# An MLP over q and the routing of a mixture of experts: fixed instruction orders, a halved last group, and a first load in two parts

## The chip, the cores and the metric

The kernel runs on one core of one Trainium2 chip. A core has a matrix engine (TensorE, PE in the profile), a vector engine (VectorE, DVE), an engine for activation functions (ScalarE, ACT), a general engine (GpSimd, POOL) that here mostly issues indirect transfers, and a sync engine (SyncE, SP) that issues plain transfers. Each engine runs its own list of instructions in order, and the engines wait for one another by semaphores. The metric is the device time in microseconds (us), from launch to end, and less is better. All data are float32.

## The reference

The reference is two layers of a network on x of 8 x 512 tokens of 128 values, thus 4096 tokens: a convolution stage, a feed-forward stage with quantized values, a stage that trains a small MLP on the keys and applies it to the queries, and a mixture of experts. The change touches the end of the third stage and the beginning of the fourth:

```
h_q = swish(q @ gate) * (q @ val)              # hidden size 512
x = x + h_q @ proj @ proj_w + proj_b
xt = layernorm(x).reshape(T, 128)
logits = xt @ Wg + bg                          # 8 experts
gate_vals, exp_idx = top_k(softmax(logits), 2)
gate_vals = gate_vals / sum(gate_vals)
eidx = exp_idx.T.reshape(-1)
oh = one_hot(eidx, 8)
pos = sum((cumsum(oh, axis=0) - oh) * oh, axis=-1)
keep = pos < 1229                              # the capacity of one expert
buf[eidx, pos] += where(keep, xt, 0)           # rows of the first choices of all tokens come first
h = gelu(einsum("ecd,edf->ecf", buf, W1) + b1)
ye = einsum("ecf,efd->ecd", h, W2) + b2
x = x + sum over the two choices of ye[eidx, pos] * gate_vals * keep
```

A row's place in its expert's buffer depends on how many earlier tokens chose that expert; rows of second choices are placed from the other end, so that one count per expert is enough.

## The kernel before

The kernel runs `sequence_conv`, `fp4_ffn`, `ttt` and `moe` one after the other. Tokens lie in tiles of P = 128; G = 4 tiles are a group of W = 512 columns, and there are NG = 8 groups. The last part of `ttt` (L853 to L877), "the MLP on q", loops over the groups. For each of NF = 4 chunks of the hidden size it has two matmuls into PSUM buffers of 512 columns, `pa` (L857) and `pb` (L861), of which there are four; ScalarE makes silu of `pa` into `sw` (L865, two buffers) and VectorE the product into `ht` (L866). These are called chunk 0 to chunk 3 here. Then sixteen matmuls of 128 columns, four chunks into each of the group's four tiles, make the output `o` (L872), and VectorE adds it to x (L876, "the x add").

Between the products and the output of group g stands `moe.route(g - 1)` (L1198 to L1288), the routing of the group before; the last group's routing follows the loop (L877). A route has these parts:

- turn: four transposes of x (L1212), copied to `xt` by ScalarE (L1214)
- statistics: `bn_stats` and `bn_aggr` by tile (L1217, L1218), then `rsqrt` by a bit trick and three Newton steps (13 small VectorE operations, L85 to L93)
- logits: four matmuls of 8 columns (L1224), made into `lg` on VectorE (L1226, L1227)
- rows: the normalized tokens into `xr` (ScalarE, L1231), with a copy for the second choice (VectorE, L1252)
- choices: for each of the two, five operations that find the best expert and its one-hot `hot` (L1237 to L1241); the tanh of the difference gives both weights (L1247 to L1250)
- counts: `hot` is counted up over the group's tiles into `cum`, starting from `seen`, the count of all earlier groups (L1254 to L1260); this is what ties each route to the one before it
- sums: two matmuls over the partitions (L1261, L1262) into `pos`, which shares a PSUM tile named `both` with the logits
- places: seven operations that turn the sums into row numbers `slot` (L1263 to L1273)
- scatters: eight indirect transfers on POOL (L1278), one for each tile and choice, second choices (k = 1) before first ones (k = 0). Each k = 0 scatter waits until the k = 1 scatters of the route before have landed (`self.after`, L1286).

The eight scatters of one route are called a train here. `Moe.experts` (L1297) then goes over the E = 8 experts: SP loads an expert's nine full row tiles in one transfer and its last, ragged tile in another (L1333, L1337), both after all scatters; then transposes (L1356), a copy (L1358), first matmuls `ph` (L1362), Gelu (L1365), second matmuls `po` (L1371), the results (L1380, L1384) and the scatter of results (L1386).

In which order an engine runs its instructions is not written out in this part: the compiling framework places every instruction on its engine by its own plan, so that parts of a route stand between the products and outputs of the loop. A class `Line` is there already (it keeps the instructions handed to it in the order of the calls, without a semaphore), and other stages use it; this part does not.

Of the kernel before, what the change touches and what calls it, by code (L numbers as in the profile page):

```python
# [1 line left out]

# [14 lines left out]
P = 128  # L17
# [706 lines left out]
def ttt(cx):  # L724
# [10 lines left out]
    with ExitStack() as st:  # L735
# [106 lines left out]
        with ExitStack() as s4:  # L842
# [10 lines left out]
            for g in range(NG):  # L853
                ht = p2.tile([P, NF, W], F32, tag="ht", name="ht")
                for c in range(NF):
                    pa = ps_h.tile([P, W], F32, tag="h", name="pa")
                    nc.tensor.matmul(  # L857
                        pa, gate[:, c * P : (c + 1) * P], qt[:, g * W : (g + 1) * W], start=True, stop=True
                    )
                    pb = ps_h.tile([P, W], F32, tag="h", name="pb")  # L860
                    nc.tensor.matmul(  # L861
                        pb, val[:, c * P : (c + 1) * P], qt[:, g * W : (g + 1) * W], start=True, stop=True
                    )
                    sw = p2.tile([P, W], F32, tag="sw", name="sw")
                    nc.scalar.activation(sw, pa, AF.Silu)  # L865
                    nc.vector.tensor_tensor(ht[:, c, :], pb, sw, ALU.mult)  # L866
                if g:
                    moe.route(g - 1)
                o = ps_o.tile([P, G, D], F32, tag="o", name="o")
                for j in range(G):  # L870
                    for c in range(NF):
                        nc.tensor.matmul(  # L872
                            o[:, j, :], ht[:, c, j * P : (j + 1) * P], w2[:, c, :],
                            start=(c == 0), stop=(c == NF - 1),
                        )
                nc.vector.tensor_tensor(grp(cx.x, g), o, grp(cx.x, g), ALU.add)  # L876
            moe.route(NG - 1)  # L877
# [251 lines left out]

class Moe:  # L1130
# [67 lines left out]
    def route(self, g):  # L1198
        cx = self.cx
        nc, tc, p2 = cx.nc, cx.tc, self.p2  # L1200
        vec = nc.vector

        def small(tag, *shape, dt=F32):
            return p2.tile([P, *shape], dt, tag=tag, name=tag)

        def over_e(t):
            return t.unsqueeze(2).to_broadcast([P, G, E])

        x, at = grp(cx.x, g), slice(g * G, (g + 1) * G)
        tp = self.ps_t.tile([P, G, P], F32, tag="t", name="tp")  # L1210
        for j in range(G):
# [234 lines left out]
```

## Time and profile before

| | us |
|---|---|
| median of three runs (lowest, highest) | 1364.11 (1363.63, 1365.26) |
| the profiled execution | 1367.42 |
| its span, first to last instruction | 1365.7 |
| TensorE, VectorE, ScalarE, POOL busy in the whole span | 1122.8, 776.2, 493.7, 761.5 |
| mean granted TensorE clock of the span | 0.927 |

One row of the page's list of the costliest groups bears on the part in question, and so does its line of the granted clock:

```profile
PEclk9888899976999999999999999999999886899996
...
L1278 POOL DMA_INDIRECT rows<-xr,slot x64 | 62.4, 976 | 104.9 <-DVE rs L93 55.6
```

A row reads: line, engine, operation, output and inputs by the program's names, count; then busy time in all and mean ns of one; then the idle time just ahead of the group on its engine and what ended most of it. The clock line has 40 slices of 34 us; a digit is the clock that TensorE was granted, in tenths of full speed. The slices of the part that the change touches read 9, 8, 8, 6, 8, between two rows of nines near the right end: in the trace it runs from 1004 us, when the loop over the groups begins, to 1167 us, when the first expert's rows have landed.

A row of the timeline gives start and duration in us, engine, line, operation and shapes, with count, and in brackets the idle time ahead of it and what ended it.

### The profile page before, as it was taken

To read this page: it belongs to the slowest core of one execution; us is meant where nothing else is said; L and a number is where in the kernel's file an instruction comes from. 1 tells how busy PE (TensorE), PEld (TensorE's weight loads), DVE (VectorE), ACT (ScalarE), POOL (GpSimd) and SP (SyncE) were. 2 spreads that over 40 slices of the span, in tenths; PEclk is the share of its full clock that TensorE was granted. 3 is DMA by queue.
4 is the path that set the end of the run, shared out by engine and by line. 5 is a ranking of instruction groups with operands and counts; after the bars stand their busy time and mean duration, and the time that the engine had idled before them with its cause. 6 is when DMAs were issued, how large, how long until landed. Compare 5 with 4: busy or idle time off the path is not lost.

```text
span 1365.7 us, 15325 instructions
## 1 busy us (share of the span) xinstructions
PE 1122.8 (82%) x5211; PEld 661.2 (48%) x5211; DVE 776.2 (57%) x1754; ACT 493.7 (36%) x1002; POOL 761.5 (56%) x724
## 2 busy tenths in 40 slices
PE   4688888726878689999998999999898873799981
PEld 1233333314656445555556455555665442576761
DVE  8689899978796544444445444444556564122233
ACT  4534455325555632222234222222442221333320
POOL 4336566644554588888841888888104336244533
PEclk9888899976999999999999999999999886899996
DMA  4322223924000000000000000000000001222146
GB/s 133 90 73 73 73 73 95 348 82 143 1 0 1 0 0 1 0 0 1 1 1 1 1 0 1 0 1 1 0 1 30 24 28 43 57 60 63 48 114 182
DMA packets 61614, 63.07 MB, mean 46 GB/s; under 512 B 6767, under 2 KB 44478, under 8 KB 61536
## 3 DMA queue, kind: packets, MB, share of 16 engines
q1 hardware_dynamic: 54016, 52.37, 13.1%
q0 software_dynamic: 4608, 8.43, 2.0%
q10 hardware_dynamic: 2912, 1.29, 0.4%
q8 instruction: 41, 0.67, 0.2%
q14 instruction: 37, 0.30, 0.1%
HBM read 37.90 MB, written 25.04 MB: 46 GB/s over the span
## 4 chain that ended last, share of the span: by engine, by line
issue 62%; PE 10%; DMA 2%; DVE 1%; SPq 1%; POOL 1%; POOLq 0%; ACT 0%; another core or an unknown queue 0%; DVEq 0%
PE po L1371 5%; PE ph L1362 5%; DMA w<-in_L_ffn_W 1%; POOL last L1386 1%; DMA y<-last 1%; PE tp L1356 0%; POOLq L1442 0%; DVE ye L1380 0%; DVE xt L1358 0%; DMA xe<-rows 0%; DMA L_ffn_bg<-in_L_ffn_bg 0%; SPq L604 0%; SPq L710 0%; DMA last<-ye,tok 0%; SPq L59 0%
## 5 line engine op out<-in xcount | busy, mean ns | idle before, releaser
L1051 POOL TENSOR_TENSOR ds<-sw,s 128x512 f32<-128x512 f32 x64 | 81.4, 1272 | 86.7 <-DVE sw L1046 86.7
L1278 POOL DMA_INDIRECT rows<-xr,slot x64 | 62.4, 976 | 104.9 <-DVE rs L93 55.6
L1386 POOL DMA_INDIRECT res<-ye,xe x70 | 68.2, 974 | 89.6 <-DVE ye L1384 36.3
L1053 POOL TENSOR_TENSOR ds<-ds,s 128x512 f32<-128x512 f32 x64 | 112.1, 1751 | 5.0
L391 PE MATMUL cv<-pr,sel 128*32 128x512 f32 x512 | 78.4, 691 | 22.5 <-DVE pr L381 22.4
L1044 ACT COPY b<-pb 128x512 f32<-128x512 f32 x64 | 37.4, 585 | 162.1 <-PE pb L1040 161.6
L1365 ACT ACTIVATE ht<-ph,b 128x512 f32<-128x512 f32 (+1 forms) x96 | 55.5, 602 | 107.9 <-PE ph L1362 96.5
L1048 DVE TENSOR_TENSOR h<-sw,b 128x512 f32<-128x512 f32 x64 | 50.2, 784 | 70.6 <-ACT b L1044 70.1
L1371 PEld LDWEIGHTS po<-w,ht 128*128 128x128 f32 (+1 forms) x640 | 79.5, 193 | 15.3 <-issue 9.5
L1052 POOL TENSOR_TENSOR ds<-sw,ds 128x512 f32<-128x512 f32 x64 | 82.5, 1289 | 5.0
L1371 PE MATMUL po<-w,ht 128*128 128x128 f32 (+1 forms) x640 | 83.0, 284 | 2.7 <-ACT ht L1365 2.6
L1054 POOL TENSOR_TENSOR ds<-ds,b 128x512 f32<-128x512 f32 x64 | 81.4, 1271 | 5.0
L1076 PEld LDWEIGHTS pp<-proj,ht 128*128 128x128 f32 x512 | 67.1, 191 | 30.7 <-issue 29.8
L1362 PE MATMUL ph<-xt,w 128*128 128x512 f32 (+1 forms) x192 | 73.9, 522 | 9.6 <-DVE xt L1358 7.6
L383 POOL TENSOR_TENSOR pr<-base,en 128x512 f32<-128x512 f32 x48 | 69.6, 1479 | 21.7 <-ACT en L345 21.7
L381 DVE TENSOR_TENSOR pr<-base,w 128x3072 f32<-128x3072 f32 x24 | 79.6, 3318 | 2.5 <-ACT w L343 2.5
L1380 DVE TENSOR_TENSOR ye<-po,b 128x512 f32<-128x512 f32 (+2 forms) x32 | 14.9, 488 | 112.7 <-PE po L1371 87.1
L1046 DVE TENSOR_TENSOR sw<-pa,s 128x512 f32<-128x512 f32 x64 | 44.2, 691 | 53.6 <-ACT s L1042 53.6
L1071 ACT COPY ht<-pt 128x512 f32<-128x512 f32 x64 | 37.4, 585 | 101.6 <-PE pt L1069 101.6
L1086 PE MATMUL ph<-proj_t,dpt 128*128 128x512 f32 x128 | 71.6, 641 | 0.0
L1088 DVE TENSOR_TENSOR db<-ph,sw 128x512 f32<-128x512 f32 x64 | 44.2, 691 | 47.4 <-PE ph L1086 47.4
L1038 PE MATMUL pa<-gate,kt 128*128 128x512 f32 x128 | 66.8, 604 | 2.5 <-ACT b L1044 2.4
(320 smaller groups left out, 2665.0 us busy)
## 6 DMA issues: line engine op xcount, KB each, us to landing
base<-far SPq DMA_DIRECT2D x64, 268.0 KB
rows<-empty SPq DMA_DIRECT2D x1, 5005.0 KB
xe<-rows SPq DMA_DIRECT2D x8, 585.0 KB
res<-zero SPq DMA_DIRECT2D x1, 4096.0 KB
w<-in_L_ffn_W SPq DMA_DIRECT2D x16, 256.0 KB
y<-res SPq DMA_DIRECT2D x16, 256.0 KB
far<-avg SPq DMA_DIRECT2D x8, 272.0 KB
x<-in_L_attn_x SPq DMA_DIRECT2D x8, 256.0 KB
```

Of the source, the lines that this page charges most:

```text
L381: vec(nc.vector.tensor_tensor(pr[:, :nv, :], s["base"][:, :nv, at], w.to_broadcast([P, nv, L]), ALU.mult))
L383: nc.gpsimd.tensor_tensor(pr[:, d, :], s["base"][:, d, at], s["en"][:, g, :], ALU.mult)
L391: ten(nc.tensor.matmul(s["cv"][32 * j : 32 * (j + 1), :], sel[:, i].rearrange("p a h -> p (a h)"), s["pr"][g][:, i * NJ + j, :], start=(g ...
L1051: nc.gpsimd.tensor_tensor(ds, sw, s, ALU.mult)
L1052: nc.gpsimd.tensor_tensor(ds, sw, ds, ALU.subtract)
L1053: nc.gpsimd.tensor_tensor(ds, ds, s, ALU.add)
L1054: nc.gpsimd.tensor_tensor(ds, ds, b, ALU.mult)
L1076: nc.tensor.matmul(pp, ht[:, c * P : (c + 1) * P], proj[:, c, :], start=(c == 0), stop=(c == NF - 1))
L1086: nc.tensor.matmul(ph, dpt, proj_t, start=True, stop=True)
L1362: nc.tensor.matmul(ph[:, :n], self.w1[:, e, c * P : (c + 1) * P], xt[:, :n], start=True, stop=True)
L1371: nc.tensor.matmul(po[:m, i - c0, :], ht[:, c, at : at + m], self.w2[:, e, c, :], start=(c == 0), stop=(c == NF - 1),)
L1386: sc = nc.gpsimd.indirect_dma_start(out=(self.slots.last if last else self.slots.res)[:, :], out_offset=bass.IndirectOffsetOnAxis(ap=num[: ...
```

## The change

- The loop and the routing get fixed orders: three `Line`s, one for VectorE, TensorE and ScalarE. `Moe.route` becomes a class `Route` whose parts are methods; those on VectorE are generators, and `run` goes through one or several of them in turn, one instruction of each. The parts of the old group's route are called between the chunks of the new group: turn and statistics behind chunk 0, logits and roots behind chunk 1, rows and the first choice behind chunk 2, the second choice behind chunk 3, counts and sums between the two halves of the outputs, places before the x add.
- `sw` has three buffers for two. The logits have a PSUM tile of the transposes' pool, apart from `pos`.
- Four operations of a route go from VectorE to ScalarE: the copy of the rows, the copy of `hot`, and the two that write the weights. `bn_stats` of all tiles come before `bn_aggr` of all.
- The last group is cut in two halves of two tiles, each with its own route. At the end the rest of the first half's route and the second half's route run in alternation.
- The k = 0 scatters no longer wait for the k = 1 scatters of the route before by four dependences each; a small memset on POOL (`gate`) waits for them, and the k = 0 scatters stand behind it on POOL.
- At the end ScalarE gets a Gelu of one column (`ahead`).
- The first expert's nine row tiles are loaded in two transfers, of four and five tiles.

```diff
--- before.py
+++ after.py
...
+            vec, ten, act = Line(tc), Line(tc), Line(tc)
+            parts = [(g * G, G) for g in range(NG - 1)] + [(NT - G, G // 2), (NT - G // 2, G // 2)]
+            def hidden(lo, n, c):
+                at = slice(lo * P, (lo + n) * P)
+                ps = []
+                for w in (gate, val):
+                    ph = ps_h.tile([P, W], F32, tag="h", name="ph")[:, : n * P]
+                    ten(nc.tensor.matmul(ph, w[:, c * P : (c + 1) * P], qt[:, at], start=True, stop=True))
+                    ps.append(ph)
+                sw = p2.tile([P, W], F32, tag="sw", name="sw", bufs=3)[:, : n * P]
+                act(nc.scalar.activation(sw, ps[0], AF.Silu))
+                return ps[1], sw
+            def gated(ht, c, pb, sw):
+                vec(nc.vector.tensor_tensor(ht[:, c, : pb.shape[1]], pb, sw, ALU.mult))
+            def out_of(o, ht, lo, hi):
+                for j in range(lo, hi):
                     for c in range(NF):
+                        ten(nc.tensor.matmul(
                             o[:, j, :], ht[:, c, j * P : (j + 1) * P], w2[:, c, :],
                             start=(c == 0), stop=(c == NF - 1),
+                        ))
+            old = None
+            for lo, n in parts:
+                final = lo + n == NT
+                ht = p2.tile([P, NF, W], F32, tag="ht", name="ht")
+                o = ps_o.tile([P, G, D], F32, tag="o", name="o")
+                h = hidden(lo, n, 0)
+                if old:
+                    old.turn()
+                    run(old.stats())
+                gated(ht, 0, *h)
+                h = hidden(lo, n, 1)
+                if old:
+                    old.logits()
+                    run(old.roots())
+                gated(ht, 1, *h)
+                h = hidden(lo, n, 2)
+                if old:
+                    old.normal()
+                    run(old.first())
+                gated(ht, 2, *h)
+                h = hidden(lo, n, 3)
+                if old and not final:
+                    run(old.second())
+                gated(ht, 3, *h)
+                out_of(o, ht, 0, n // 2)
+                if old and not final:
+                    run(old.before())
+                    old.sums()
+                out_of(o, ht, n // 2, n)
+                if old and not final:
+                    run(old.places())
+                x = cx.x[:, lo : lo + n, :]
+                vec(nc.vector.tensor_tensor(x, o[:, :n, :], x, ALU.add))
+                new = Route(moe, lo, n, vec, ten, act)
+                if final:
+                    new.turn()
+                    new.logits()
+                    run(chain(new.stats(), new.roots()), chain(old.second(), old.before()))
+                    old.sums()
+                    new.normal()
+                    run(new.first(), old.places())
+                    run(chain(new.second(), new.before()))
+                    new.sums()
+                    run(new.places())
+                old = new
+            ahead = wp.tile([P, 1], F32, tag="ahead", name="ahead")
+            act(nc.scalar.activation(ahead, cx.eps[1e-5], AF.Gelu_apprx_tanh))
...
+def run(*chains):
+    chains = list(chains)
+    while chains:
+        chains = [c for c in chains if next(c, chains) is not chains]
+class Route:
+    def __init__(self, moe, lo, n, vec, ten, act):
+        self.moe, self.lo, self.n, self.vec, self.ten, self.act = moe, lo, n, vec, ten, act
+        self.x = moe.cx.x[:, lo : lo + n, :]
+        self.rows = [moe.xr[:, k, lo : lo + n, :] for k in range(K)]
+        self.rank = moe.rank[:, :n, :]
+    def small(self, tag, *shape, dt=F32):
+        return self.moe.p2.tile([P, *shape], dt, tag=f"{tag}{self.n}", name=tag)
+    def over_e(self, t):
+        return t.unsqueeze(2).to_broadcast([P, self.n, E])
+    def turn(self):
+        m, nc = self.moe, self.moe.cx.nc
+        tp = m.ps_t.tile([P, W], F32, tag="t", name="tp")[:, : self.n * P]
+        for j in range(self.n):
+            self.ten(nc.tensor.transpose(tp[:, j * P : (j + 1) * P], self.x[:, j, :], m.cx.ident))
+        self.xt = self.small("xt", self.n * P)
+        self.act(nc.scalar.copy(self.xt, tp))
+    def stats(self):
+        vec, n = self.moe.cx.nc.vector, self.n
+        st, self.mv = self.small("st", n, 6), self.small("mv", n, 2)
+        for j in range(n):
+            yield self.vec(vec.bn_stats(st[:, j, :], self.x[:, j, :]))
+        for j in range(n):
+            yield self.vec(vec.bn_aggr(self.mv[:, j, :], st[:, j, :]))
+    def roots(self):
...
+        yield self.vec(vec.scalar_tensor_tensor(self.off, self.mv[:, :, 0], -1.0, rs, ALU.mult, ALU.mult))
+    def normal(self):
+        nc, rows = self.moe.cx.nc, self.rows
+        for j in range(self.n):
+            self.act(nc.scalar.activation(
+                rows[0][:, j, :D], self.x[:, j, :], AF.Identity, bias=self.off[:, j : j + 1], scale=self.rs[:, j : j + 1]
+            ))
+        self.act(nc.scalar.copy(rows[1][:, :, :D], rows[0][:, :, :D]))
+    def logits(self):
+        m, nc = self.moe, self.moe.cx.nc
+        pl = m.ps_t.tile([P, W], F32, tag="t", name="pl")[:, : self.n * E]
+        self.pl = pl.rearrange("p (j e) -> p j e", e=E)
+        for j in range(self.n):
+            self.ten(nc.tensor.matmul(self.pl[:, j, :], self.xt[:, j * P : (j + 1) * P], m.w_c, start=True, stop=True))
+    def choose(self, k):
...
+    def first(self):
+        m, vec, n = self.moe, self.moe.cx.nc.vector, self.n
...
+        yield from self.choose(0)
+        yield self.vec(vec.scalar_tensor_tensor(flat(lg), flat(self.hot[:, 0]), -1e30, flat(lg), ALU.mult, ALU.add))
+    def second(self):
+        nc = self.moe.cx.nc
+        dif = self.small("dif", self.n)
+        yield from self.choose(1)
+        self.act(nc.scalar.copy(self.hot[:, K], self.hot[:, K - 1]))
+        yield self.vec(nc.vector.tensor_tensor(dif, self.best[:, 0, :], self.best[:, 1, :], ALU.subtract))
+        self.act(nc.scalar.activation(dif, dif, AF.Tanh, scale=0.5))
+        for k, s in enumerate((0.5, -0.5)):
+            self.act(nc.scalar.activation(self.rows[k][:, :, D + 1], dif, AF.Copy, bias=0.5, scale=s))
+    def before(self):
+        m, vec, n, hot = self.moe, self.moe.cx.nc.vector, self.n, self.hot
+        self.cum = cum = self.small("cum", K + 1, n, E)
+        last = m.seen
+        for j in range(n):
+            yield self.vec(vec.tensor_copy(cum[:, :K, j, :], last)) if j == 0 else self.vec(
+                vec.tensor_tensor(cum[:, :K, j, :], cum[:, :K, j - 1, :], hot[:, :K, j - 1, :], ALU.add)
+            )
+        yield self.vec(vec.tensor_tensor(m.seen, cum[:, :K, n - 1, :], hot[:, :K, n - 1, :], ALU.add))
+        yield self.vec(vec.tensor_tensor(
+            cum[:, K], cum[:, K - 1], m.seen[:, 0:1, :].to_broadcast([P, n, E]), ALU.add
+        ))
+    def sums(self):
+        m, nc, n = self.moe, self.moe.cx.nc, self.n
+        pos = m.ps_r.tile([P, 4 * G * E], F32, tag="r", name="pos")[:, : (K + 1) * n * E]
+        self.pos = pos.rearrange("p (k j e) -> p k j e", k=K + 1, e=E)
+        self.ten(nc.tensor.matmul(self.pos, m.before, self.hot, start=True, stop=False))
+        self.ten(nc.tensor.matmul(self.pos, m.ones, self.cum, start=False, stop=True))
+    def places(self):
+        m, nc, n, rk = self.moe, self.moe.cx.nc, self.n, self.rk
+        tc, vec, lo = m.cx.tc, nc.vector, self.lo
+        r, room, slot = self.small("r", K + 1, n), self.small("room", K, n), self.small("slot", K, n, dt=I32)
+        yield self.vec(vec.tensor_tensor(self.cum, self.pos, self.hot, ALU.mult))
+        yield self.vec(vec.tensor_reduce(r, self.cum, AX.X, ALU.add))
+        yield self.vec(vec.tensor_scalar(room, r[:, ::2, :], float(CAP), None, ALU.is_lt))
+        yield self.vec(vec.tensor_scalar(r[:, 1, :], r[:, 1, :], -1.0, CAP - 1.0, ALU.mult, ALU.add))
+        yield self.vec(vec.scalar_tensor_tensor(flat(rk), flat(rk), -float(PITCH), flat(r[:, :K, :]), ALU.mult, ALU.add))
+        yield self.vec(vec.tensor_tensor(rk, rk, room, ALU.mult))
+        yield self.vec(vec.tensor_scalar(slot, rk, float(R), None, ALU.add))
+        new = []
+        for k in (1, 0):
+            if k == 0 and lo:
+                gate = nc.gpsimd.memset(self.small("gate", 1), 0.0)
+                m.after(gate, m.scatters[-1][: len(m.scatters[-1]) // K])
+            for j in range(n):
+                sc = nc.gpsimd.indirect_dma_start(
+                    out=m.slots.rows[:, :],
+                    out_offset=bass.IndirectOffsetOnAxis(ap=slot[:, k, j : j + 1], axis=0),
+                    in_=self.rows[k][:, j, :], in_offset=None, bounds_check=m.limit, oob_is_err=False,
+                )
+                tc.declare_no_dep(sc.ins, group="scatter", reason="order kept by gates")
+                tc.add_to_no_dep_group("scatter", sc.ins)
+                if k == 0 and lo:
+                    after(tc, sc, gate, sync=False)
+                new.append(sc.ins.name)
+        m.scatters.append(new)
...
-    def route(self, g):
...
                 last = e == E - 1
                 full = base + (NR - 1) * P
                 rows = self.slots.rows
-                self.after(
-                    nc.sync.dma_start(
-                        out=xe[:, : NR - 1, :], in_=rows[base:full, :].rearrange("(n p) d -> p n d", p=P)
-                    ), every,
-                )
+                for lo, hi in ((0, G), (G, NR - 1)) if e == 0 else ((0, NR - 1),):
+                    src = rows[base + lo * P : base + hi * P, :].rearrange("(n p) d -> p n d", p=P)
+                    self.after(nc.sync.dma_start(out=xe[:, lo:hi, :], in_=src), every)
                 self.after(nc.sync.dma_start(out=xe[:left, NR - 1, :], in_=rows[full : base + CAP, :]), every)
                 num = xe[:, :, D : D + 1].bitcast(I32)
                 if last:
```

## What is predicted, and from what

> **What bounds the kernel now.** The span by line puts the change in one stretch, 1004 to 1167 us. The page's chain of waits is no help there (62% is "issue"), so I read the waits of that stretch, then a timeline of one group, then two-microsecond windows. Waits (engine, line, what ended the wait: us in total, times, longest):
>
> ```profile
> DVE x L876 <- remote: 18.2, 5, 4.5
> ACT sw L865 <- remote: 17.6, 4, 5.0
> PE both L1261 <- DVE hot L1244: 15.6, 4, 4.2
> ```
>
> "Remote" means that the profile knows no releaser. One group's timeline tells more (start, us, engine, line, work, idle before):
>
> ```profile
> 1052.52 2.70 PE L872 MATMUL o<-w,ht 128*128 128x128 f32 x22
> 1055.06 1.02 PE L857 MATMUL pa<-qt,gate 128*128 128x512 f32 x2
> ...
> 1057.73 0.97 POOL L1278 DMA_INDIRECT rows<-xr,slot  x1 [0.30 <-issue]
> 1060.34 0.69 DVE L876 TENSOR_TENSOR x<-o,x 128x512 f32<-128x512 f32 x1 [4.48 <-remote]
> 1060.44 0.60 ACT L865 ACTIVATE sw<-pa 128x512 f32<-128x512 f32 x1 [5.00 <-remote]
> 1061.70 1.97 PE L857 MATMUL pa<-qt,gate 128*128 128x512 f32 x2
> ```
>
> The matmuls of o end at 1055.22, those of pa at 1056.08. Their readers, on two engines, start together at 1060.34 and 1060.44: 1.64 us after the eighth and last scatter of that route (1057.73 + 0.97 = 1058.70). In four of the steady groups it is the same, 1.60 to 1.72 us after the last scatter. So **TensorE's results raised late in a train of scatters are seen only behind it**. The windows show the second price (PE, PEld, DVE, ACT, POOL busy, then TensorE's clock, DMA share, GB/s):
>
> ```profile
> 1058.00:1060.00 2.00, 0.00 (x0) 0.00 (x0) 0.00 (x0) 0.00 (x0) 0.70 (x1) 0.83 0.21 67
> 1060.00:1062.00 2.00, 0.83 (x3) 0.83 (x4) 1.66 (x11) 0.60 (x1) 0.00 (x0) 0.50 0.00 0
> ```
>
> TensorE stood still and its clock is halved until about 1066; the pa pair takes 1.97 us, not 1.02. The x adds (L876) start at 1015.95, 1027.79, 1042.92, 1060.34, 1079.62, 1098.86, 1117.54 and 1136.46: a steady group takes 19.0 us, though by the same rows TensorE needs 12.4, VectorE 12.9 and POOL 10.2.
>
> The end of the stretch, by the timeline:
>
> ```profile
> 1149.25 0.17 DVE L1273 TENSOR_SCALAR slot<-rk 128x8 int32<-128x8 f32 x1 [0.19 <-DVE rk L1271]
> 1160.36 0.97 POOL L1278 DMA_INDIRECT rows<-xr,slot  x1 [0.30 <-issue]
> 1162.78 0.46 SPq L1333 DMA_DIRECT2D xe<-rows  x1
> 1167.22 1.94 PE L1356 MATMUL tp<-ident,xe 128*128 128x128 f32 x8 [19.47 <-DMA xe<-rows]
> ```
>
> After the last x at 1136.46 the last slots take 13.0 us, but POOL's 16 scatters of routes 6 and 7 run in one row from 1141.21 to 1161.33, then the load lands 4.3 us after its issue. TensorE and VectorE do nothing from 1150 to 1167.
>
> **The change, part by part.**
>
> *Operations moved from VectorE to ScalarE.* Per group: copy L1252 0.44, two of L1250 0.39, L1244 0.18: about 1.0 us less on VectorE. ScalarE is busy 43.6 us of the 174 that I windowed; it takes about 1.2 us more per group beside free time. If the cover is gone, silu is late by one copy, 0.6 us.
>
> *The fixed lines.* Counted from the end of the fourth gated product (t0): the counting before the sums is 6 VectorE operations of about 0.19 = 1.1; the remaining 10 of 16 passes of out's first half at 0.1155 and the sums at 0.5 to 0.6 end at 1.9; seven operations of places (1.63 in the trace) give the slots at 3.55, the first scatter T at 3.75, x from 3.6 to 4.3. TensorE meanwhile: second half of out to 3.65, chunk 0 (4 passes of 0.43 = 1.72), turn 0.44, chunk 1, logits 0.91: raised at 8.4, which is T+4.65. Then chunk 2 is raised at T+5.5 and T+6.4, chunk 3 at T+7.3 and T+8.2. VectorE behind the logits: first (8 operations, 1.7), gated 0.69, second (2.0 with gaps), gated 0.69: t0 again at **13.65**. Its own sum and TensorE's 12.4 are both under it, so nothing else binds. 13.7 against 19.0.
>
> *Price of late signals, not shown for this order.* Lower end: 0. Upper end: chunk 2, raised at T+6.4, is seen at 11.55 (eight scatters 1.275 apart, ending at 9.9, plus 1.64): 5.2 us per group. Nearest row for the logits, which bind first, is this one, in the train that began at 1087.34:
>
> ```profile
> 1090.93 1.06 PE L1224 MATMUL both<-w_c,xt 128*128 128x8 f32 x8
> ...
> 1093.01 0.19 DVE L1226 TENSOR_TENSOR lg<-both,rs 128x32 f32<-128x32 f32 x1 [2.85 <-PE both L1224]
> ```
>
> Raised at train+4.65, seen 1.02 late. I take **1.0 us per group**, and the same for later chunks, since in the expert stage's train of ten from 1306.69 signals at +5.4 to +8.9 came 0.3 to 1.6 late, not at its end. Period 14.7.
>
> The Trainium skill ("TensorE: Matmul & The Clock Gate", Part 1: The HAM clock gate) says that an idle window of about 3.4 us brings half clock. The windows agree: 4.2 idle before L1261, then 0.50. By my sum TensorE idles from T+8.7 to about T+10.9, so the rule costs nothing; with a hold to the train's end it idles over 5 us, and the rule adds about 1.9 (half-clock passes of out 1.15 and sums 0.5 to 0.6). This is the rule that speaks against the change.
>
> *Other edits of the loop.* A third sw buffer, the logits' own PSUM tile and inlined roots take no time of their own. A POOL memset replaces four waits of the k=0 scatters; it stands in the built order behind the previous train and costs nothing beside trains that leave POOL 3.5 us free; without that cover about 0.2. Slot writes wait for scatters of two routes earlier, long done.
>
> *Last group as two halves.* Half A: passes half as wide and gated products 0.35 for 0.69, 13.7 - 1.4 = 12.3. Half B: also without second, before and places of A (4.7), with smaller operations: 8.3. Then B's x 0.35, 43 VectorE operations of the two alternating chains at 0.22 = 9.5, sums and waits 1.4: slots 11.3 after B's x starts. Four scatters follow alone: 3 x 1.275 + 0.97 = 4.8, issue 0.3. So 16.4 from x to the last scatter's end, before 24.9.
>
> *First load.* SP issues two parts, 4 and 5 of 9 row tiles (266 and 333 KB), for one of 599 KB; the second and the ragged one are behind it on SP's queue, and needed only after 4 transposes and four half passes, over 3 us later. The skill's page "DMA: Bandwidth & Descriptors" (Anatomy of one DMA) gives 2.0 us fixed plus bytes over 436e3, so the fixed part isn't split: an estimated 0.76 saved. The row has 4.30 for 599 KB, 0.93 above that rule; 2.3 us that scale give 4.30 - 3.02 = 1.28. I take 1.2. Bounds: 0 (parts share the engines) and 1.3. The early table load for Gelu (1.28 before the first Gelu) I put at 0: TensorE is at its own matmuls until 1174.24; bounds 0 and 0.4.
>
> **The sum.** First x 1015.95 as before; second 1029.6 (its group gains nothing: no route stood in group 0); five more of 13.7: 1098.1; A 1110.4; B 1118.7; last scatter's end 1135.1. Before: 1161.3. Saved 26.2 + 1.2 = 27.4: **1340.0** of the execution's own 1367.4, or 1336.7 of the median 1364.1 (the profiled one is 3.3 longer). Late signals at 1.0 in five groups, A and B: +7. Forecast **1344**.
>
> **The rivals.**
> - *No hold* (20%): in this order signals are taken at once: 1337. For it: VectorE's and ScalarE's own signals were never held. Against: 1.02 above.
> - *My case* (42%): lags of 1 to 2 us, up to a release at train+8.7 as in the first train (o, raised at +5.8): 1.3 more for five groups and A, plus some slow clock: 1340 to 1357.
> - *Hold to the end of the train, with half clock* (30%, slower): chunk 2 seen at T+11.55, period 18.9, and 1.9 for the clock: 19.5 to 20.8. Then the seventh x at 1127 to 1134, A and B 27 to 30 later, 17 to the end, less 1.2: 1373 to 1388. It decides from the point where 27.4 is eaten: 6.3 periods' worth, 13.7 + 4.3 = **18.0 us**. For it: the two "remote" rows, same scatters, same position. Against: the first train, the expert train, and that chunk 2 now stands before nothing that is held with it.
> - *Hold without the clock* (8%): period near 18, the halves give the rest back: 1362 to 1367. No change is anything within 0.2%, 2.7 us.
> That the orders are not kept I leave out: the built program has all three lines as written.
>
> Own range of the likeliest: 1340 to 1357. The range, 1334 to 1377, holds the first two, the fourth and the lower third of the third. Faster 0.62, same 0.08, slower 0.30.
>
> **What would show it.** The spacing of the x adds: 14 to 15.5 for me, 13.7 for no hold, over 18 for the slower rival. "Remote" waits of the product and of silu, and the clock in windows: 0.50 in mid-loop would be the rival. The last scatters: end 16 to 17 us after the last x, only four alone. First load: landing about 3 us after issue. I am wrong if the product of chunk 2 starts 1.6 us after each last scatter.

## The result, and the profile after

The changed kernel takes **1344.75 us** in the median of four runs (1341.90 to 1346.14), beside 1364.68 us for the kernel before in the same runs (four, 1363.63 to 1367.83). The ratio is 0.9847, with a 95% interval from 0.9824 to 0.9871: 1.5% faster. In a second comparison it was 1346.05 against 1365.4 us, ratio 0.9866 (0.9846 to 0.9886).

In three sets of runs the kernel before took 1364 to 1365 us, in two others 1329 us, so each kernel is compared only with the runs of the kernel before in its own set. In all eight traces from the former, TensorE's results come late behind trains of scatters; in the six from the latter they don't. I call the two kinds of sets "with holds" and "without holds". The two main comparisons above are both with holds.

The page of the changed kernel has these rows for the ones shown of before (the clock line, then the scatters):

```profile
PEclk8799899987899989999999999999999996899996
...
L1325 POOL DMA_INDIRECT rows<-xr,slot x64 | 62.4, 976 | 82.8 <-PE o L876 35.6
```

A slice is 33.5 us here. The loop, 1005 to 1125 us, now lies in nines up to 1106 us; a single 6 is left at its end, where the two halves of the last group run. The scatters cost POOL the same 62.4 us as before, so what was won is waiting time.

One group of the timeline of the changed kernel shows where the waiting still is (start, us, engine, line, work, idle before). It begins with the first scatter of a train, then the last pass of chunk 3 and the product that reads it, then the last scatter:

```profile
1087.17 0.97 POOL L1325 DMA_INDIRECT rows<-xr,slot  x1 [4.15 <-DVE x L913]
...
1093.22 1.02 PE L864 MATMUL ph<-qt,val 128*128 128x512 f32 x2
1095.49 0.68 DVE L871 TENSOR_TENSOR ht<-ph,sw 128x512 f32<-128x512 f32 x1
1096.11 0.97 POOL L1325 DMA_INDIRECT rows<-xr,slot  x1 [0.30 <-issue]
1097.65 0.39 PE L1304 MATMUL pos<-cum,ones 128*128 128x96 f32 x2
1098.99 0.26 DVE L1310 TENSOR_TENSOR cum<-pos,hot 128x96 f32<-128x96 f32 x1 [1.62 <-PE pos L1304]
1100.46 0.17 DVE L1317 TENSOR_SCALAR slot<-rk 128x8 int32<-128x8 f32 x1 [0.24 <-DVE rk L1316]
1100.54 0.68 DVE L913 TENSOR_TENSOR x<-o,x 128x512 f32<-128x512 f32 x1
1101.39 0.97 POOL L1325 DMA_INDIRECT rows<-xr,slot  x1 [4.20 <-DVE x L913]
```

The sums end at 1098.04 and are seen at 1098.99, 0.95 us later and 1.91 us behind the end of the last scatter (1097.08). In the first route of the same trace, with no train ahead of it, the sums are seen 0.11 us after their end. VectorE waits 1.62 us for them here. From there it is 1.64 us to the slots and 0.76 to the first scatter of the next train. So the loop is a ring: a train of 9.91, 1.91 until the sums are seen, 1.64 + 0.76 = 14.22 us, and this x add comes 14.22 us after the one before it (1086.32). The windows of the same time (busy us of PE, PEld, DVE, ACT, POOL, then the clock, DMA share, GB/s) show that the clock stays at 1.00 through these gaps:

```profile
1095.00:1097.00 2.00, 0.78 (x7) 0.77 (x7) 1.79 (x10) 0.63 (x4) 1.70 (x2) 1.00 0.20 67
1097.00:1099.00 2.00, 2.00 (x20) 2.00 (x19) 0.34 (x3) 0.00 (x0) 0.19 (x2) 1.00 0.10 33
```

At the end of the stretch, the last scatter, the two loads (SP's own queue) and the first transposes of the experts:

```profile
1140.23 0.97 POOL L1325 DMA_INDIRECT rows<-xr,slot  x1 [0.30 <-issue]
1142.85 0.93 SPq L1450 DMA_DIRECT2D xe<-rows  x2
1145.83 2.29 PE L1470 MATMUL tp<-ident,xe 128*128 128x128 f32 x8 [12.63 <-DMA xe<-rows]
```

That is 2.98 us from the issue to the first transpose; before it was 1167.22 - 1162.78 = 4.44.

| from the traces, us | before | changed | predicted |
|---|---|---|---|
| first x add to the seventh | 101.6 | 83.9 | 87.2 |
| seventh x add to the end of the last scatter | 43.8 | 40.7 | 39.0 |
| end of the last scatter to the first transpose of the experts | 5.9 | 4.6 | 4.7 |
| first hidden matmul to the first transpose ("the stretch") | 162.8 | 140.3 | |
| from there to the end | 198.5 | 194.4 | |

The spans differ by 25.5 us: 22.5 in the stretch, 4.1 behind it, and 1.1 lost ahead of it, where nothing was changed. The medians differ by 19.9 us only, since the trace of before is of a run 2.7 us above its median and this one of a run 2.9 us below. The 4.1 can't be put down to the change: most of it lies in the last expert, where the last two blocks of transposes started 7.5 us apart in the trace of before and 3.6 in this one, and in a second trace of the changed kernel 6.2. The part behind the stretch varies with the holds too: it takes 192.0 to 193.0 us in the six traces without holds and 194.4 to 199.6 in the eight with them. The experts have rows of scatters of their own.

### The profile page after: what moved, and what is told of

It is laid out like the page before. It is cut to its first block, busy times and chain, and to the rows that moved or that the text cites. A ratio compares the mean times of both kernels' runs of the same rounds, so it can differ in the third digit from the quotient of the medians.

```text
span 1340.2 us, 15404 instructions
## 1 busy us (share of the span) xinstructions
PE 1113.9 (83%) x5231; PEld 659.8 (49%) x5231; DVE 785.5 (59%) x1764; ACT 503.4 (38%) x1045; POOL 761.6 (57%) x732
## 4 chain that ended last, share of the span: by engine, by line
PE 52%; DVE 12%; ACT 4%; issue 4%; POOL 4%; DMA 1%; POOLq 0%; DVEq 0%; SPq 0%; ACTq 0%; another core or an unknown queue 0%
PE po L1485 5%; PE ph L1476 5%; PE ph L1137 5%; PE sum L1112 4%; PE pp L1127 4%; PE sum L1111 4%; PE sum L1113 4%; PE pa L1089 4%; PE pb L1091 4%; PE pt L1120 2%; PE gu L644 2%; PE o L876 1%; POOL v L571 1%; DVE ht L871 1%; PE ph L864 1%
## 5 line engine op out<-in xcount | busy, mean ns | idle before, releaser
L1325 POOL DMA_INDIRECT rows<-xr,slot x64 | 62.4, 976 | 82.8 <-PE o L876 35.6
L1485 PE MATMUL po<-w,ht 128*128 128x128 f32 (+1 forms) x640 | 80.2, 278 | 2.0 <-ACT ht L1479 1.9
L1122 ACT COPY ht<-pt 128x512 f32<-128x512 f32 x64 | 37.4, 585 | 101.6 <-PE pt L1120 101.6
```

The lines of the kernel that those rows point to most:

```text
L1485: nc.tensor.matmul(po[:m, i - c0, :], ht[:, c, at : at + m], self.w2[:, e, c, :], start=(c == 0), stop=(c == NF - 1),)
```

## The experiments

All were run beside the kernel before. "Period" is the mean distance of the x adds from the second to the seventh.

| | us | before in its set | period | the stretch |
|---|---|---|---|---|
| before | 1364.68 | | 17.95 | 162.8 |
| changed | 1344.75 | 1364.68 | 14.09 | 140.3 |
| the same again | 1346.05 | 1365.4 | 14.11 | 140.9 |
| one load, no early Gelu | 1344.64 | 1364.48 | 14.16 | 141.4 |
| last group whole | 1341.88 | 1364.48 | 14.13 | 140.4 |
| no fixed orders | 1344.07 | 1364.48 | 14.37 | 140.6 |
| ninth scatter | 1349.60 | 1364.48 | 15.48 | 149.1 |
| before, x add behind the slots | 1366.46 | 1365.4 | 19.06 | 162.5 |
| *without holds:* the same | 1333.56 | 1329.46 | 13.67 | 134.7 |
| five scatters | 1332.20 | 1329.46 | 13.55 | 134.0 |
| before, two scatters | 1326.57 | 1329.46 | 12.70 | 128.0 |
| train in two fours | 1334.39 | 1329.46 | 13.58 | 135.5 |
| the same again | 1333.41 | 1329.40 | 13.58 | 135.7 |
| sums early | 1343.73 | 1329.40 | 15.08 | 145.0 |

**One load and no early Gelu.** Two small parts of the change are taken back.

```diff
-                for lo, hi in ((0, G), (G, NR - 1)) if e == 0 else ((0, NR - 1),):
+                for lo, hi in ((0, NR - 1),):
...
-            act(nc.scalar.activation(ahead, cx.eps[1e-5], AF.Gelu_apprx_tanh))
```

> The changed kernel with the first expert's rows in one load again and without the early Gelu of one column. Theory: the load in two parts brought the first rows 2.95 us after the issue against 4.30, so here they land 1.3 to 1.4 us later; without the early table load the first Gelu is late by up to 1.3 us, of which TensorE's own matmuls hide most. In all 1.4 to 2.2 us slower than the changed kernel, 1346 to 1347. Rival: the parts share the same engines and the gain in landing is eaten by a later second part: no difference, 1345, with the first expert's results at the same distance from the last scatter.

From the issue to the first transpose it takes 4.31 us again, against 2.98: the split load is worth 1.3 us in the trace. The medians, 1344.64 and 1344.75, don't show it, and the 1346 to 1347 of the theory were not met; runs of one kernel differ by 4 us. Of the early Gelu nothing can be said: from the first transpose to the second block of them it took 15.0 us here and 13.9 in the first trace of the changed kernel, but 15.2 in the second one.

**The last group whole.**

```diff
-            parts = [(g * G, G) for g in range(NG - 1)] + [(NT - G, G // 2), (NT - G // 2, G // 2)]
+            parts = [(g * G, G) for g in range(NG)]
```

> The changed kernel with the last group whole (its route runs in alternation with the rest of the route before, as the halves do). Theory A, the halves are worth something, as the prediction's 8.3 + 16.4 us has it: from the seventh x add (1100.5 us in the changed kernel) to the end of the last scatter it takes 40.7 us with halves, and more with the whole group: 14.2 + 24.9 = 39 to 43 by the rows of the kernel before. Theory B, at the end POOL's sixteen scatters are the bound and in the halved version POOL sits idle for 6 us between trains: with the whole group the x add comes 10.5 us after the seventh, slots of route 6 some 6 us later, then sixteen scatters in one row, 20.1: 37 us, 3 to 4 us faster than the changed kernel, 1341.

From the seventh x add to the end of the last scatter: 12.5 + 28.2 = 40.8 us, against 40.7 with halves (41.4 in the second trace of the changed kernel). The halves are worth nothing that can be seen. Theory B was right that sixteen scatters then run in one row (20.15 us), but they start 8.1 us after the last x add and not 6, and that x add comes 12.5 us after the one before and not 10.5. The median, 1341.88, lies lower than that of the changed kernel, but the runs of the two overlap (1340.1 to 1346.8, 1341.9 to 1346.1), and their stretches are equal.

**No fixed orders.** All else of the change stays.

```diff
-            vec, ten, act = Line(tc), Line(tc), Line(tc)
+            vec = ten = act = lambda ins: ins
```

> The changed kernel without the three fixed orders: each engine's order is left to the planner again, all other edits stay. Theory: the order brought the loop from 19.0 to 14.2 us a group; without it x adds wait behind trains again, period 17 to 19, five to six groups: 15 to 28 us slower, 1360 to 1372, with granted clock 0.50 inside the loop. Rival: the operations moved to ScalarE, the third sw buffer and the logits' own PSUM tile did it: period 14 to 15, 1345 to 1349.

The theory falls: 1344.07 us and a period of 14.37. One group, of a train from 1074.63 to 1084.55:

```profile
1080.38 0.83 PE L876 MATMUL o<-w,ht 128*128 128x128 f32 x6
1081.05 1.02 PE L864 MATMUL ph<-qt,gate 128*128 128x512 f32 x2
1082.41 0.59 ACT L867 ACTIVATE sw<-ph 128x512 f32<-128x512 f32 x1
...
1084.35 0.46 PE L1304 MATMUL pos<-cum,ones 128*128 128x96 f32 x2
1086.33 0.26 DVE L1310 TENSOR_TENSOR cum<-pos,hot 128x96 f32<-128x96 f32 x1 [1.78 <-PE o L876]
1087.47 0.68 DVE L913 TENSOR_TENSOR x<-o,x 128x512 f32<-128x512 f32 x1
```

The planner, with the program rewritten as it is, puts each route's counts and sums ahead of the x add by itself. What the change brought is in the order of the program and the other edits, not in the lines that pin it. The period that the rival named came. Whether the order of the program did it, or the operations moved to ScalarE, the third `sw` buffer or the logits' own PSUM tile, no run separates.

**A ninth scatter** behind each train of a full route, to DRAM that nobody reads.

```diff
+        if n == G:
+            spare = m.slots.dram.tile([R, DX], F32, tag=f"spare{lo}", name="spare")
+            sc = nc.gpsimd.indirect_dma_start(
+                out=spare[:, :],
+                out_offset=bass.IndirectOffsetOnAxis(ap=slot[:, 0, n - 1 : n], axis=0),
+                in_=self.rows[0][:, n - 1, :], in_offset=None, bounds_check=m.limit, oob_is_err=False,
+            )
+            after(tc, sc, last, sync=False)
```

> The changed kernel with a ninth scatter behind each train of a full route, into DRAM that nobody reads; results are unchanged. Theory: in the changed loop the sums are seen 1.7 to 1.9 us after the end of the last scatter of the train before, so the period is 9.9 (train) + 1.9 + 1.6 (places) + 0.75 = 14.2, a cycle through the train: a ninth scatter makes it 15.5, and 1.28 us more for each of five groups, half A and the end: 1352 to 1354. Rival: VectorE's own work sets the period, and POOL with 9 x 1.275 = 11.5 of 14.2 us has room: loop unchanged, x adds 14.2 apart, 1345 to 1346.

The period is 15.48, 1.39 more than 14.09, for one scatter of 1.275. The time, 1349.60 us, lies between what the theory (1352 to 1354) and the rival (1345 to 1346) had named, so the verdict rests on the period. The timeline of this kernel, one group, from the first scatter of a train to the ninth at 1070.86 and beyond:

```profile
1060.63 0.97 POOL L1325 DMA_INDIRECT rows<-xr,slot  x1 [4.26 <-DVE x L913]
...
1069.58 0.97 POOL L1325 DMA_INDIRECT rows<-xr,slot  x1 [0.30 <-issue]
1070.86 0.97 POOL L1338 DMA_INDIRECT spare<-xr,slot  x1 [0.30 <-issue]
1071.12 0.39 PE L1304 MATMUL pos<-cum,ones 128*128 128x96 f32 x2
1073.83 0.26 DVE L1310 TENSOR_TENSOR cum<-pos,hot 128x96 f32<-128x96 f32 x1 [2.98 <-PE o L876]
```

The sums end at 1071.51, 10.88 us after the train's first scatter, as in the changed kernel (10.87); they are now seen 2.32 us late, 2.00 behind the end of the ninth scatter. POOL had room for it (11.2 of 15.5 us), VectorE waited longer. So, with holds, the ring through the train is the bound of the changed loop, and the rival, VectorE's own pace, is out.

**Five scatters, two scatters, a train in fours.** These were to show what the loops do when the train is short or broken. The first two leave rows out. The edits are, in this order, five scatters in the changed kernel, two in the kernel before, and the four k = 0 scatters held back behind the third product in the changed kernel.

```diff
-            for j in range(n):
+            for j in range(G - 1 if k and n == G else 0, n):
...
-            for j in range(G):
+            for j in range(1 if g < NG - 1 else G):
...
+                p = gated(ht, 2, *h)
+                if older:
+                    older.scatter(0, p)
```

> The changed kernel with five scatters for each full route in place of eight: the rows of the second choice of three tiles of each group are left out (later results that need them are left out with them). Theory, the loop is a cycle through the train: the train takes 6.1 us, the cycle 6.1 + 1.9 + 2.4 = 10.4, so it no longer binds, and VectorE's and TensorE's own work does: x adds 13.0 to 13.5 us apart, the sums seen at once; 5 to 7 us faster in the loop, some 1338 to 1341. Rival, the lag of the sums has nothing to do with scatters (TensorE's own pace, the wait of its matmuls): period 14.2 as in the changed kernel.

> The kernel before with two scatters for each route but the last, in place of eight: the rows of three of four tiles are left out. Theory: the 19 us of its groups are a train of 9.9, 1.65 until TensorE's results are seen, and 7.7 from the x add to the next slots; with two scatters (2.2 us) nothing is held, x adds 13 to 14.5 apart, no wait with an unknown releaser at the x add, clock 1.00 in mid-loop, 1333 to 1342 in all. Rival: the waits at the x add come from the order of TensorE's and VectorE's instructions and not from scatters: x adds stay 18 to 19 us apart.

> The changed kernel with each route's train in two: four scatters of second choices at once, the four of first choices only when the next group's third gated product is done, some 2 us after the first four. All eight are issued, and results are unchanged. Theory 1, what holds TensorE's results is a train without a gap from about its sixth microsecond on: the sums are raised 3 to 4 us into the second four, are seen at once, and the period is VectorE's own, 13.0 to 13.6: 1339 to 1341. Theory 2, any scatters in flight hold them until 1.9 us after the last: the second four end later, at 12.3 us after the first scatter, and the period is 12.3 + 1.9 + 2.4 = 16.6: 1356 to 1360.

All three fell on a set without holds: the kernel before itself took 1329.46 us beside them. So they tell the pace of each loop when nothing is held, and no more: the changed kernel's is 13.5 to 13.6 us a group, with five scatters or eight in fours, and that of before 12.7 with two scatters. What theory and rival said of holds they leave open. From the third route on, the second four of a route also ran straight into the first four of the next, so that version has rows of eight again. The train in fours was run again in the hope of a set with holds:

> The changed kernel with each route's train in two fours with a gap, once more, for the case that the kernel before takes some 1364 us beside it (its first run fell on a set of runs in which nothing was held). There the sums are raised some 10.9 us after the first scatter, 3 us into the second four (7.4 to 12.2). Theory 1, results are held in a long train alone, and a four holds them by 0.95 us at most as in the expert stage: x adds 13.5 to 14.0 apart, 1339 to 1344. Theory 2, they are held until 1.7 to 1.9 us after the last scatter, however the scatters are grouped: x adds 16 to 16.7 apart, 1354 to 1360. Where the kernel before takes some 1329: 13.5 again, 1334.

It met the other kind again, with 1333.41 us where 1334 was named for that case, against 1329.40, ratio 1.0030 (1.0022 to 1.0038).

**The kernel before with the x add behind the slots**, as one added order on VectorE.

```diff
-        vec.tensor_scalar(slot, rk, float(R), None, ALU.add)
+        self.placed = vec.tensor_scalar(slot, rk, float(R), None, ALU.add)
...
+                ad = nc.vector.tensor_tensor(grp(cx.x, g), o, grp(cx.x, g), ALU.add)
+                if g:
+                    after(tc, ad, moe.placed, sync=False)
```

> The kernel before with one order added: on VectorE the x add of a group stands behind the slots of the route before (no semaphore, nothing else is changed by hand; the planner places the rest around it). Theory: the change gained in the loop because counts, sums and places no longer stand behind the held x add on VectorE; so this one order brings the period from 19.0 to 14.4 to 15.5, as a train of 9.9, 1.65 to 1.9 and what follows: 1341 to 1349. Rival: the operations moved to ScalarE, the third sw buffer and the logits' own PSUM tile are needed for it: 1355 to 1364.

> The kernel before with the x add behind the slots of the route before on VectorE, once more. Theory: on a chip that holds results behind a train, the period is 9.9 + 1.65 to 1.9 + what follows, 14.4 to 16, against 19.0 of the kernel before, 1341 to 1351 us against 1364; on a chip that holds nothing, as in the first run of it, 1332 to 1335 against 1329. Rival on the first kind of chip: other edits are needed, 1355 to 1364.

The first run was without holds: 1333.56 us. The second was with holds, and there the theory falls: 1366.46 against 1365.4 us, ratio 1.0005 (0.9990 to 1.0019), period 19.06. The x add no longer stands in the way, but other results do. The waits of this run, from 1005 to 1150 us (us in total, times, longest):

```profile
ACT sw L865 <- remote: 12.2, 3, 5.1
DVE ht L866 <- remote: 11.3, 2, 5.9
DVE lg L1228 <- remote: 1.2, 1, 1.2
```

One group of its timeline, of a train from 1083.33 to 1093.23:

```profile
1086.26 2.25 PE L872 MATMUL o<-w,ht 128*128 128x128 f32 x18
...
1088.35 1.02 PE L861 MATMUL pb<-qt,val 128*128 128x512 f32 x2
1089.21 1.02 PE L857 MATMUL pa<-qt,gate 128*128 128x512 f32 x2
...
1092.26 0.97 POOL L1280 DMA_INDIRECT rows<-xr,slot  x1 [0.30 <-issue]
1095.01 0.69 DVE L866 TENSOR_TENSOR ht<-pb,sw 128x512 f32<-128x512 f32 x1 [5.41 <-remote]
1095.04 0.60 ACT L865 ACTIVATE sw<-pa 128x512 f32<-128x512 f32 x1 [5.04 <-remote]
1095.75 2.07 PE L861 MATMUL pb<-qt,val 128*128 128x512 f32 x2 [3.80 <-DVE ht L866]
```

A product and a silu, on two engines, start together 1.8 us behind the last scatter; TensorE has stood for 3.8 us, and its next pair takes 2.07 us for 1.02. It is what the kernel before showed with the x add, one step on. In the set without holds the same program does the same work in its train from 1057.88, and nothing waits for an unknown releaser:

```profile
1061.14 2.92 PE L872 MATMUL o<-w,ht 128*128 128x128 f32 x24
...
1064.76 1.02 PE L861 MATMUL pb<-qt,val 128*128 128x512 f32 x2
...
1066.19 0.68 DVE L866 TENSOR_TENSOR ht<-pb,sw 128x512 f32<-128x512 f32 x1
```

Here pb ends at 1065.78, 7.9 us after the first scatter, and is used 0.4 us later, with the train still running.

The traces also keep the time of each semaphore update, and that tells whether the signal is late or only its reader. Without holds, every signal that TensorE raises in the train above is recorded 0.01 to 0.02 us after its matmul's end. With holds, the signals of the five passes that end from 1088.52 to 1091.95 are recorded from 1094.87 to 1095.04, one every 0.04 us. So the signals themselves arrive late, in one burst. The same lists show one more difference. In the eight traces with holds 6 to 11% of VectorE's updates are missing, all of them in the loop, the routing and the experts; in the six without holds none is. Whether the holds come from the recording itself, or the losses and the holds have one cause, no run here tells.

**The changed kernel again.**

> The changed kernel itself, beside the kernel before, because the two chips of the experiments so far gave the kernel before 1364.5 and 1329.5 us. Theory: whether TensorE's results are held behind a train depends on the chip. On a chip where the kernel before takes some 1364 us this one takes 1344 to 1345, with x adds 14.2 apart; on a chip where it takes some 1329 nothing is held, x adds of this one come 13.5 apart (VectorE's own pace) and it takes 1333 to 1336, slower than before by 4 to 6 us. Rival: all kernels are faster by the same amount on the second chip: 1308 to 1312 there.

A set with holds: 1346.05 against 1365.4, period 14.11. The time of this set is 1 us above the theory's 1344 to 1345, its period is met. The second half of the theory, that the changed kernel is the slower one where nothing is held, was not run for this kernel itself. Its version with trains in fours was, twice, at 0.3% over the kernel before. One set of each kind carries the same chip number in its record, so the chip alone is not the reason, if that number stands for one chip.

**Sums early.**

```diff
                     run(old.second())
+                    run(old.before())
+                    old.sums()
                 gated(ht, 3, *h)
-                out_of(o, ht, 0, n // 2)
...
+                out_of(o, ht, 0, n)
```

> The changed kernel with counts and sums one step earlier: counts ahead of the fourth gated product on VectorE, sums ahead of all output matmuls on TensorE. Slots are then ready, and the train starts, while the output matmuls still run. Theory 1, what is raised behind a block of output matmuls that runs inside a train is held until 1.7 us after its last scatter: the sums come ahead of that block and are seen at once, but the x add and the next group's first chunk fall into the new train and are held, as in the kernel before: x adds 17 to 20 apart, 1355 to 1372. Theory 2, only the last microseconds of a train hold: sums seen at the train's end as before, places at once behind them: x adds 13.5 to 14.2 apart, 1340 to 1345. Where the kernel before takes some 1329 and nothing is held: 12.8 to 13.3, 1329 to 1333.

Without holds again, and slower than expected there: 1343.73 against 1329.40 us, periods of 14.4 to 16.1. VectorE, done with the slots, waits 1.9 to 3.5 us for the output matmuls that now start later. Which results of a train are held, which this run was to tell, stays open.

## Why the prediction was right, and where it was not

The forecast was 1344 us, from a sum that saved 27.4 and gave 7 back to late signals; 1344.75 was measured. In the spans the changed kernel gained 22.5 us in the stretch, where the sum had 20.4. That the two times lie within 1 us is luck: against the sum the loop came out 3.3 us shorter and the end 1.7 longer, and the medians gained 19.9 where the traces gained 22.5 in the stretch alone.

The first point below needs one more line of the kernel before, the first scatter behind the x add at 1060.34:

```profile
1068.06 0.97 POOL L1278 DMA_INDIRECT rows<-xr,slot  x1 [9.36 <-DVE slot L1273]
```

- **The mechanism was right, if drawn too wide.** Some of TensorE's results raised late in a train are seen only behind it, though not all (below), and the loop's length hangs on what stands behind the held result. The ring of the kernel before is 9.9 + 1.65 + 7.7 (the x add at 1060.34 to the next train at 1068.06) = 19.2; that of the changed one is 9.9 + 1.9 + 2.4 = 14.2. The 5.3 us between 7.7 and 2.4 are counts, sums and other work that no longer follow a held result, most of it at half clock. The ninth scatter shows that the ring binds.
- **The size of the lag was right, its place and its price wrong.** I put 1.0 us a group on the logits, raised at train + 4.65. They are raised at train + 3.5 and are there before VectorE asks; the sums, which I took as free, are 0.6 to 1.3 us late. In the period that costs 0.5 to 0.6 and not 1.0, since the versions of this loop without holds have 13.5 to 13.6 against 14.1. I had the first scatter 0.2 us after the slots and ahead of the x add; it comes 0.76 us after them, behind the x add's start. A period of 14.7 was predicted, 14.1 measured; the pace without holds was 13.65 by my count.
- **"The fixed lines" as the cause was wrong.** Under that name I costed the new order, and the run without the lines has nearly the same period (14.37 for 14.09) and the same time.
- **The halves were mis-sized.** Half A took 14.0, not 12.3: it too waits for held sums (2.1 us, at 1113.02). Half B took 10.2, not 8.3 (and 12.3 less the 4.7 left out would be 7.6): VectorE stands 3.3 us ahead of its x add, whose matmuls are seen 0.96 us late, and the last twelve of them take 2.59 us at a clock of 0.50. At the pace of the full group (ten in 1.38 us) they would take about 1.7, an estimate. The 16.4 from there to the last scatter's end was met (16.43). Together 40.7 for 37.0, or for 39.0 with the late signals, and the whole group does it in 40.8.
- **The split load** saved 1.3 to 1.5 us in the traces, 1.2 was taken. The rule of the Trainium skill's page "DMA: Bandwidth & Descriptors" (Anatomy of one DMA), with 0.76 saved, was too low, as it already was by 0.93 for the whole load. The page gives it for the path of GpSimd; this load is issued by SP, so the rule was used outside what it states.
- **The clock** stayed at 1.00 through the seven full groups, as the sum had it: TensorE's longest pause there is 1.2 us. It fell in the halves, which the sum had not: to 0.50 from 1108 to 1115 us and again from 1122. The prediction took an idle window of about 3.4 us as what brings half clock. In the 3.4 us ahead of these two drops TensorE was busy for 1.59 and 1.40 us (1.64 and 1.44 in the second trace of this kernel), and its longest pause was 1.5. So here TensorE did not have to be idle throughout.
- **The slower rival** had a hold to the train's end with half clock. Its mechanism is real: the kernel before with the x add late is just that, period 19.06. It didn't meet the changed order, whose third and fourth chunks, raised at train + 5.4 to + 7.1, were taken within 1.3 us in the train from 1087.17. Why those are not held and others at the same place are is not settled. In the groups shown of the kernel before and of the run with the x add late, 22 and 18 output matmuls, as the trace counts them, run inside the train up to the held results; in the changed kernel output matmuls come only after these chunks. An output block alone isn't enough: in the run without fixed orders six of them stand in the train ahead of a pass that ends at 1082.07, at train + 7.4, and silu reads it 0.34 us later. The number of matmuls in the train may decide, but that is argued, not shown. Its time was also summed too high at the upper end: 1134 + 30 + 17 is 19.7 us behind 1161.3, which less 1.2 gives 1383 from the median, and not 1388.
- **What no case held:** that the holds can be absent. Then the kernel before takes 1329 us, 35 less. Six groups at 12.7 in place of 18 would make 32 of it, an estimate that gives them the pace of the run with two scatters; the kernel before itself has no trace without holds. The gain of the change is then gone: its version in fours is 4 to 5 us slower than the kernel before, about the 4.5 that five groups at 13.6 in place of 12.7 would cost.

Only the kernel before with the x add late was run in both kinds of sets, and it gained in neither. With holds the last group whole (1341.88) is as good as the changed kernel and simpler; without them the kernel before was ahead of all versions run there that leave nothing out.

## What to carry to other kernels

Where several engines idle until the same moment, look for what ended just before it on an engine that has nothing to do with them; here it was a row of scatters on POOL. A loop like this one is a ring: write down what must happen between the late event and the next start of the thing that made it late, and shorten that. Here the work moved ahead of the late event fitted in beside the train, and pinning the order added nothing that could be measured. Measure the kernel before beside every run, since the cost that a change removes may not be there in the next set of runs.

## What was not expected of the hardware

- TensorE's results are held behind scatters in some sets of runs and not in others, with the same program: 1366.46 and 1333.56 us for the kernel before with the x add late. The kernel before took 1365 and 1329 us in the same sets. With holds the traces also lack semaphore updates; the cause of both is open.
- The hold ends 1.6 to 2.0 us behind the end of the last scatter, whether that is the eighth or the ninth, and results raised at different times are then seen within 0.1 us of each other (1060.34 and 1060.44; 1095.01 and 1095.04).
- Results of VectorE and ScalarE were not seen to be held in any trace read here: in the train from 1087.17, TensorE starts on a product of VectorE 0.06 us after its end, at train + 9.1.
- The clock fell to 0.50 after 3.4 us in which TensorE was busy for 1.4 to 1.6 us.
- From the issue of the load to the first transpose it takes 4.3 to 4.4 us with 599 KB in one, 2.8 to 3.0 with the first 266 KB of two.
